# Sums of the down weights: from VectorE in one run to GpSimd in two, in the first block of a macaron layer

## The chip, the core and the metric

The kernel runs on one core of one Trainium2 chip. A core has TensorE (PE: matrix products into PSUM), VectorE (DVE), ScalarE (ACT) and GpSimd (POOL) for element-wise work, and SyncE (SP), whose queue issues every DMA of this kernel. Each engine works through its own instructions in the order in which they were written and waits on semaphores for the others. The metric is the device time of one execution in microseconds (us), lower is better; one other execution was taken with the hardware profiler.

## What is computed

Eight sequences of 512 tokens of width 512 pass through a gated feed-forward, attention, and the feed-forward again, each behind a layer norm and added to its input:

```python
x = x + 0.5 * ffn(layernorm(x));  x = x + attention(layernorm(x));  x = x + 0.5 * ffn(layernorm(x))

h = silu(x @ w_gate) * (x @ w_up)          # 512 -> 2048
h_sparse = the two of each four neighbours of h that are largest in magnitude
ffn = h_sparse @ w_down                    # 2048 -> 512
```

All of it is float32. The weights are the same for the sixteen feed-forwards.

## The kernel before

The work is cut into 16 blocks, one feed-forward of one sequence each. A block makes the hidden units in four parts (`c` = 0 to 3), and each part in two pairs (`i` = 2c and 2c + 1). A pair is seven products of eight matmuls (`woven`, L583): a Strassen-like scheme with seven products in place of eight, that works on four weight quarters (`Q11`, `Q12`, `Q21`, `Q22`) and on four sums of them (`S1` to `S4`). The very first pair is made plainly (`hidden`, L563). Three PSUM banks go round. Around the products, VectorE adds banks into a row and a corner (L608), multiplies (L157, the line of a helper that runs anything put off), and picks two of four (`keep_two_of_four`, L363 to L421), whose sums over halves of h (`e`) GpSimd makes (L415 to L420).

Two parts of h then go through the down weights with another seven products (`products`, L504), of sixteen matmuls each. These need, for each half `g` of the down weights, two quarters as they are and five sums of quarters (`SUMS`, L453). The sums are made once, in the first block: `combine_down` loads 1 MB of raw down weights, makes five sums of 128 x 512 float32, and writes each to memory (tile `wd`), four times over (`c` = 0 to 3; two times for each `g`). All later blocks read them from there (`down_weights`, L482). In the same way `combine_gu` (L656) makes `S1` to `S4` of the gate and up weights on VectorE, in the first block only, and stores them (tile `gu`).

The order of the instructions is written by a planner at build time. It keeps a modelled clock for PE, DVE and ACT (`at`), puts VectorE work into three queues (`urgent`, `put_off`, `for_later`), and after each product `fill` runs what fits by its estimate. GpSimd and DMAs have no clock in it. Side work (layer norms, attention, `combine_down`) is a generator that is advanced step by step between two places of the main work, given in half-products of 512 columns: the tuple for `combine_down` is (first place, last place, steps, ...), L960. The counter starts at 6.5 (L981); the first pair takes 4 places, every other pair 3.5, and a product with the down weights 1. Numbered from 0, pair 1 runs from 10.5, pair 2 from 14, pair 3 from 17.5, pair 4 from 21 and pair 5 from 24.5, with the first two down products woven in; the other five follow, and pair 6 begins at 35. `raw` lies in a ring of two buffers (`p_slots`), `sums` in one buffer (`wa_slots`), and the weight quarters `w` in a ring of sixteen (`load_quarters`, L106), so that the quarters of a pair are loaded into the buffers of the pair two before it, when that is done with them. In the first block VectorE reads these new quarters for the sums of the next pair while the present pair runs.

One line says how a sum was put on VectorE, one at a time and when it fits: `made = later(0.7, partial(combine, i, name), at["pe"], for_later)` (L477).

Of the kernel before, what the change touches and what calls it, by code (L numbers as in the profile page):

```python
# [26 lines left out]
def macaron_block(  # L27
# [12 lines left out]
    nc = tc.nc  # L40
# [3 lines left out]
    NCH = w_gu.shape[0]  # L44
# [96 lines left out]
    at = {"pe": 0.0, "dve": 0.0, "act": 0.0}  # L141
    urgent, put_off, for_later = deque(), deque(), deque()

    def takes(engine, us, ready=0.0):
        at[engine] = max(at[engine], ready) + us
        return at[engine]

    def pe_heard():
        return at["pe"] + HEARD
# [13 lines left out]
    def later(us, does, ready=None, queue=put_off):  # L163
        queue.append(Later(us, does, pe_heard() if ready is None else ready, queue))
        return queue[-1]

    def soon(us, does, ready=None):

        return later(us, does, ready, urgent)

    def ensure(entries):

        for entry in entries:
            while entry.end is None:
                entry.queue[0].run()
        return max((entry.end for entry in entries), default=0.0)
# [20 lines left out]
    p_slots = Slots(pp, "p", 2)  # L197
# [3 lines left out]
    wa_slots = Slots(wap, "wa", 1)  # L201
# [145 lines left out]
    def fill(slack=HEARD):  # L347

        while True:
            steps = thin["next"]  # L350
            for queue in (urgent, put_off, for_later):
                if queue and queue[0].fits(slack):
                    queue[0].run()
                    break
            else:
                if not steps or max(at["dve"], steps[1]) + steps[0] > at["pe"] + slack:
                    return
                step()
# [73 lines left out]
    def begin(steps):  # L432
# [2 lines left out]
        thin["steps"] = steps  # L435
        thin["next"] = next(steps)

    gu_made, written = {}, {}
    owed = []
    HD2 = D // 2  # L440
# [12 lines left out]
    SUMS = ("11+22", "12-22", "21-11", "11+12", "21+22")  # L453
    combined = {
        (g, name): dram.tile([P, 4, HD2], FP, name=f"wd_{g}_{i}")
        for g in range(NCH // 2)
        for i, name in enumerate(SUMS)
    }

    def combine_down():  # L460

        for c in range(NCH):
            raw = p_slots.tile([P, 4, D], FP, "raw")
            nc.sync.dma_start(out=raw, in_=w_down[c])
            there = at["pe"] + 12.0
            yield lambda: there
            yield now
            quarter = {f"{i + 1}{j + 1}": raw[:, i::2, j * HD2 : (j + 1) * HD2] for i in range(2) for j in range(2)}
            sums = wa_slots.tile([P, 6, 2, HD2], FP, "sums")

            def combine(i, name, c=c, quarter=quarter, sums=sums):
                op = ALU.add if name[2] == "+" else ALU.subtract
                nc.vector.tensor_tensor(sums[:, i], quarter[name[:2]], quarter[name[3:]], op)
                nc.sync.dma_start(out=combined[c // 2, name][:, c % 2 * 2 : c % 2 * 2 + 2, :], in_=sums[:, i])

            for i, name in enumerate(SUMS):
                made = later(0.7, partial(combine, i, name), at["pe"], for_later)  # L477
            p_slots.used(wa_slots.used(made))
            yield now
        ensure([made])  # L480

    def down_weights(g, name):  # L482
        w = wdp.tile([P, 4, HD2], FP, tag="wd", name="wd")
        if (g, name) in combined:
            nc.sync.dma_start(out=w, in_=combined[g, name])
        else:
            i = int(name[0]) - 1
            for q in range(2):
                nc.sync.dma_start(
                    out=w[:, 2 * q : 2 * q + 2, :], in_=w_down[2 * g + q][:, i::2, i * HD2 : (i + 1) * HD2]  # L490
                )
        return w

    def ffn(b, final, last):
# [5 lines left out]
        def store(xb, ts):  # L500
            for t in ts:
                nc.sync.dma_start(out=done[t * P : (t + 1) * P, :], in_=xb[:, t, :])

        def products(hs, g):  # L504

            operands = []

            def load():
                if len(operands) < len(PRODUCTS):
                    operands.append(down_weights(g, PRODUCTS[len(operands)][1]))  # L510

            def product(i):
                name, _, quarters = PRODUCTS[i]
                y = Bank([P, 2, HD2], "y")
                for t in range(2):
                    for n in range(4):
                        h, e = hs[n // 2]
                        if name in ("11+22", "21+22", "11+12"):
                            part = e[:, ("11+22", "21+22", "11+12").index(name), n % 2, :]
                        else:  # L520
                            row, col = int(name[0]) - 1, int(name[1]) - 1
                            part = h[:, 2 * (n % 2) + col, row * HALF : (row + 1) * HALF]
                        nc.tensor.matmul(  # L523
                            out=y.tile[:, t, :],
                            lhsT=part[:, t * P : (t + 1) * P],
                            rhs=operands[i][:, n, :],
                            start=(n == 0),
                            stop=(n == 3),
                        )
                takes("pe", 3.69)  # L530
                load()
                xb = xs[b, final]

                def add(half, side, sign, ends):
                    to = xb[:, 2 * half : 2 * half + 2, side * HD2 : (side + 1) * HD2]
                    nc.vector.scalar_tensor_tensor(to, y.tile, 0.5 * sign, to, ALU.mult, ALU.add)  # L536
                    if ends and g == NCH // 2 - 1 and i >= 5:
                        store(xb, (0, 1) if i == 5 else (2, 3))

                fill()  # L540
                y.free([soon(0.62, partial(add, *to, to == quarters[-1])) for to in quarters])
                written[b, final] = y.slot[1]

            for _ in range(3):
                load()
            return [(1 if i < 2 else 2, partial(product, i)) for i in range(len(PRODUCTS))]
# [129 lines left out]
        for c in range(NCH):  # L676
# [27 lines left out]
            else:  # L704
                for pair in range(2):
                    i = 2 * c + pair
# [25 lines left out]
            if plain:  # L732
                owed.extend((1 + t // 2, partial(down, h, w_plain, c, t)) for t in range(NT))
            elif c % 2:
                owed.extend(products(hs[-2:], c // 2))
# [221 lines left out]
        return WIDTH * blocks.index((b, i))  # L957


    sides = [(9, 25, 3 * NCH, combine_down, None, None)]  # L960
    for b, i in blocks[1:]:
        stage = partial(layernorm_t, normed[b, i], "xf", tokens[b][2 * i])
        sides.append((place(b, i) - 15, place(b, i) - 2, NORM, stage, ("attention", b) if i else None, None))
# [111 lines left out]
```

## Time and profile before

| | us |
|---|---|
| median of 3 runs | 3312.73 (3311.47 to 3315.4) |
| profiled execution | 3314.09, of which the span of instructions is 3312.3 |
| PE busy | 3224.5 (97% of the span) |
| DVE busy | 2293.9 (69%) |
| ACT busy | 1368.8 (41%) |
| POOL busy | 569.4 (17%) |
| first block's sums on DVE (L473) | 20, the first at 38.9, the last at 99.0 |

The page gives busy times of each engine over the whole span. A block lasts about 207 us (3312 / 16), so a change in the first block is read from the first part of the trace: the timeline lists each engine's instructions with start, duration, and in brackets how long the engine was idle before and what ended that.

### The profile page before, as it was taken

The numbers are of one execution on the slowest core, as the hardware profiler recorded it, in microseconds if no ns is written. First come the engines' busy times: TensorE is split into PE (matmuls) and PEld (weight loads), VectorE is DVE, ScalarE is ACT, GpSimd is POOL, SyncE is SP. The second block draws the span as 40 slices with busy tenths as digits, with TensorE's granted clock in tenths as the row PEclk, the third lists the DMA queues.
The fourth block names the chain that finished last, engine by engine and source line by source line (L and its number), as shares of the span: only waits on it lengthen the run. The fifth ranks groups of instructions, "written<-read, shape, count | busy, mean of one in ns | idle before, by whom it ended". The sixth has DMA issues, their size and how long they took to land.

```text
span 3312.3 us, 43741 instructions
## 1 busy us (share of the span) xinstructions
PE 3224.5 (97%) x15880; PEld 2322.0 (70%) x15880; DVE 2293.9 (69%) x4949; ACT 1368.8 (41%) x1841; POOL 569.4 (17%) x868
## 2 busy tenths in 40 slices
PE   8899999999999999999999999998999999999999
PEld 6787657765677667766776668765676668765786
DVE  6767865686577775777668865787568765786554
ACT  2222662246424562266324652256425552266221
POOL 0222002210130022111121112120120122101120
PEclk9999999999999999999999999999999999999999
DMA  7563333542344435334453345333533436333451
GB/s 254 186 234 102 109 120 119 175 140 96 116 165 140 131 116 185 127 120 132 142 171 123 121 142 193 128 113 104 189 103 131 140 123 205 100 122 118 138 172 48
DMA packets 249285, 463.21 MB, mean 140 GB/s; under 512 B 24432, under 2 KB 64368, under 8 KB 248304
## 3 DMA queue, kind: packets, MB, share of 16 engines
q1 hardware_dynamic: 249072, 460.42, 42.3%
q8 instruction: 127, 2.08, 0.3%
q14 instruction: 86, 0.70, 0.1%
HBM read 421.53 MB, written 38.80 MB: 139 GB/s over the span
## 4 chain that ended last, share of the span: by engine, by line
PE 84%; DVE 8%; ACT 4%; DMA 2%; issue 1%; POOL 1%; SPq 0%; DVEq 0%; ACTq 0%; POOLq 0%
PE x L594 22%; PE y L523 21%; PE v L594 11%; PE z L594 6%; PE proj L760 4%; PE sc L805 4%; PE ops L854 4%; PE st L838 4%; PE y L932 3%; DMA xn<-x 1%; PE tr L239 1%; PE gu L570 1%; ACT p L846 1%; PE den L872 1%; DVE p L157 1%
## 5 line engine op out<-in xcount | busy, mean ns | idle before, releaser
L594 PE MATMUL x<-ts,w 128*128 128x256 f32 x3000 | 726.3, 385 | 12.0 <-ACT row L224 6.5
L594 PEld LDWEIGHTS x<-ts,w 128*128 128x128 f32 x3000 | 562.1, 191 | 170.9 <-issue 55.7
L523 PE MATMUL y<-wd,h 128*128 128x256 f32 x1984 | 455.8, 384 | 8.2 <-DVE h L409 5.7
L523 PEld LDWEIGHTS y<-wd,h 128*128 128x128 f32 x1984 | 374.1, 191 | 100.7 <-issue 32.6
L157 DVE TENSOR_REDUCE nm<-sc 128x1 f32<-128x512 f32 x512 | 321.6, 683 | 87.9 <-PE sc L805 86.6
L415 POOL TENSOR_TENSOR e<-h 128x512 f32<-128x512 f32 x62 | 89.9, 1450 | 1664.3 <-DVE h L409 1502.8
L231 ACT ACT_TABLE_LOAD x290 | 372.1, 1283 | 5.8 <-PEq L1064 0.7
L523 PE MATMUL y<-wd,e 128*128 128x256 f32 x1488 | 336.9, 381 | 0.6 <-POOL e L417 0.5
L536 DVE SCALAR_TENSOR_TENSOR x<-y,x 128x512 f32<-128x512 f32 x372 | 242.4, 685 | 123.1 <-PE y L523 121.4
L523 PEld LDWEIGHTS y<-wd,e 128*128 128x128 f32 x1488 | 279.5, 190 | 62.9 <-issue 22.3
L846 ACT ACTIVATE p<-st 128x2048 f32<-128x2048 f32 x128 | 238.9, 1867 | 161.8 <-DVE p L157 91.2
L224 ACT COPY row<-x 128x512 f32<-128x512 f32 x166 | 96.9, 584 | 396.9 <-PE x L594 393.4
L157 DVE TENSOR_TENSOR p<-p 128x512 f32<-128x512 f32 x384 | 254.7, 717 | 6.1 <-PE ops L854 6.0
L594 PE MATMUL v<-ts,w 128*128 128x256 f32 x1000 | 241.2, 384 | 4.3 <-DVE w L661 3.7
L594 PE MATMUL z<-xT,w 128*128 128x256 f32 x1000 | 240.2, 383 | 3.8 <-PE tr L239 2.0
L594 PE MATMUL x<-xT,w 128*128 128x256 f32 x1000 | 241.0, 384 | 0.0
L594 PE MATMUL v<-xT,w 128*128 128x256 f32 x1000 | 239.8, 383 | 0.0
L594 PEld LDWEIGHTS v<-ts,w 128*128 128x128 f32 x1000 | 187.9, 191 | 54.4 <-issue 22.4
L594 PEld LDWEIGHTS x<-xT,w 128*128 128x128 f32 x1000 | 186.7, 191 | 55.2 <-issue 27.5
L594 PEld LDWEIGHTS z<-xT,w 128*128 128x128 f32 x1000 | 187.0, 191 | 53.6 <-issue 23.3
L594 PEld LDWEIGHTS v<-xT,w 128*128 128x128 f32 x1000 | 186.7, 190 | 51.2 <-issue 12.2
L371 ACT ACTIVATE a<-h 128x1024 f32<-128x1024 f32 x128 | 134.8, 1053 | 204.4 <-DVE m L389 114.0
(108 smaller groups left out, 4068.8 us busy)
## 6 DMA issues: line engine op xcount, KB each, us to landing
w<-gu SPq DMA_DIRECT2D x472, 256.0 KB, 3.3
w<-in_w_gu SPq DMA_DIRECT2D x394, 256.0 KB, 3.3
wd<-wd SPq DMA_DIRECT2D x155, 512.0 KB, 4.0
wd<-in_w_down SPq DMA_DIRECT2D x124, 256.0 KB, 5.2
x<-x SPq DMA_DIRECT2D x64, 256.0 KB, 2.6
xn<-x SPq DMA_DIRECT2D x64, 256.0 KB, 6.6
x<-in_x SPq DMA_DIRECT2D x32, 256.0 KB, 3.3
gu<-w SPq DMA_DIRECT2D x32, 256.0 KB, 2.6
```

The lines of the kernel that those rows point to most:

```text
L157: self.does()
L231: nc.scalar.activation(dummy[:, 1:2], dummy[:, 0:1], f)
L371: nc.scalar.activation(a, h[:, :, half * HALF : (half + 1) * HALF], AF.Abs)
L523: nc.tensor.matmul(out=y.tile[:, t, :], lhsT=part[:, t * P : (t + 1) * P], rhs=operands[i][:, n, :], start=(n == 0), stop=(n == 3),)
L536: nc.vector.scalar_tensor_tensor(to, y.tile, 0.5 * sign, to, ALU.mult, ALU.add)
L594: nc.tensor.matmul(out=bank.tile[:, m, :], lhsT=lhs[:, m, k, :], rhs=rhs[:, k, :], start=(first and m == 0 and k == 0), stop=(k == 1), ski ...
L760: nc.tensor.matmul(out=ps.tile, lhsT=wa[:, k, col : col + P], rhs=xT[:, k, :], start=(k == 0), stop=(k == ND - 1))
L805: nc.tensor.matmul(out=sc[:, kv, :], lhsT=qT[rows, c, t * P : (t + 1) * P], rhs=kT[rows, :], start=True, stop=True)
L838: nc.tensor.matmul(out=st[:, kv, :], lhsT=kT[rows, t * P : (t + 1) * P], rhs=qT[rows, c, :], start=True, stop=False)
L846: nc.scalar.activation(p, st, AF.Exp)
L854: nc.tensor.matmul(out=ops[rows, :], lhsT=v[:, t, rows], rhs=p[:, kv, :], start=(t == 0), stop=(t == NT - 1))
L932: nc.tensor.matmul(out=y.tile, lhsT=qT[:, k, t * P : (t + 1) * P], rhs=wo[:, k, :D], start=(k == 0), stop=(k == ND - 1))
```

## The change

`combine_down` gets an argument `g` and makes only the two chunks of that half. It runs as two sides: the first from place 11 to 18, the second from 22 to 32. In the order that is built, the five sums of chunks 0 and 1 stand in pairs 2 and 3, those of chunk 2 in pair 5, and those of chunk 3 among the five down products after it. The sums are issued at once, five in a row, on GpSimd and no longer through VectorE's queues; each is followed by its store, on SP as before. A set `done_down` makes the build fail if a product were written ahead of its sums. Buffers and sizes stay.

```diff
-    def combine_down():
-
-        for c in range(NCH):
+    def combine_down(g):
+
+        for c in range(2 * g, 2 * g + 2):
             raw = p_slots.tile([P, 4, D], FP, "raw")
             nc.sync.dma_start(out=raw, in_=w_down[c])
             there = at["pe"] + 12.0
...
             sums = wa_slots.tile([P, 6, 2, HD2], FP, "sums")
 
-            def combine(i, name, c=c, quarter=quarter, sums=sums):
+            for i, name in enumerate(SUMS):
                 op = ALU.add if name[2] == "+" else ALU.subtract
-                nc.vector.tensor_tensor(sums[:, i], quarter[name[:2]], quarter[name[3:]], op)
-                nc.sync.dma_start(out=combined[c // 2, name][:, c % 2 * 2 : c % 2 * 2 + 2, :], in_=sums[:, i])
-
-            for i, name in enumerate(SUMS):
-                made = later(0.7, partial(combine, i, name), at["pe"], for_later)
-            p_slots.used(wa_slots.used(made))
+                nc.gpsimd.tensor_tensor(sums[:, i], quarter[name[:2]], quarter[name[3:]], op)
+                nc.sync.dma_start(out=combined[g, name][:, c % 2 * 2 : c % 2 * 2 + 2, :], in_=sums[:, i])
             yield now
-        ensure([made])
+        done_down.add(g)
...
-    sides = [(9, 25, 3 * NCH, combine_down, None, None)]
+    sides = [(11, 18, 6, partial(combine_down, 0), None, None), (22, 32, 6, partial(combine_down, 1), None, None)]
```

## The prediction

> **What bounds the kernel now.** I read first the busy times of the page, then who waited for whom on PE in the first block alone, then the timelines of PE and DVE there.
>
> ```profile
> span 3312.3 us, 43741 instructions
> PE 3224.5 (97%) x15880; PEld 2322.0 (70%) x15880; DVE 2293.9 (69%) x4949; ACT 1368.8 (41%) x1841; POOL 569.4 (17%) x868
> ```
>
> PE is the bound over the span, so only what stops PE counts. The built orders of both kernels differ in the first block alone: every engine's list is the same, line numbers aside, from the second block on. So I ask what PE loses there. The waits of PE between 24 and 142 us:
>
> ```profile
> PE y L523 <- DVE h L409: 5.7, 2, 3.0
> PE v L594 <- DVE w L661: 3.7, 1, 3.7
> PE x L594 <- DVE corner L608: 3.5, 1, 3.5
> PE z L594 <- DVE h L157: 1.7, 1, 1.7
> ```
>
> All are waits for DVE, 14.7 us together (3.52 + 1.71 + 3.73 + 2.79 + 2.96 in the PE timeline). From that timeline:
>
> ```profile
> 48.41 1.89 PE L594 MATMUL z<-xT,w 128*128 128x256 f32 x8
> 53.81 3.78 PE L594 MATMUL x<-ts,w 128*128 128x256 f32 x8 [3.52 <-DVE corner L608]
> 57.39 3.02 PE L594 MATMUL x<-xT,w 128*128 128x256 f32 x8
> 60.24 1.89 PE L594 MATMUL v<-ts,w 128*128 128x256 f32 x8
> ```
>
> After the wait eight matmuls take 3.78 and then 3.02 us, not 1.89: a wait costs more than its length. Undisturbed, eight start every 1.727 us (29.41 to 48.41 us: 19.00 / 11). From 27.69 us (pair 1) to 142.84 (first transpose in pair 6) stand 53 such eights: 39 of L594 and 14 of L523. 53 x 1.727 = 91.5 of 115.15 us, so **23.6 us are lost**: 14.7 waiting and 8.9 in slow matmuls. That is the most the change can win, 0.7%. DVE's timeline says why:
>
> ```profile
> 42.31 2.49 DVE L473 TENSOR_TENSOR sums<-raw 128x512 f32<-128x512 f32 x4
> 49.94 2.02 DVE L661 TENSOR_TENSOR w<-w 128x512 f32<-128x512 f32 x3 [5.14 <-DMA w<-in_w_gu]
> ...
> 96.55 3.10 DVE L473 TENSOR_TENSOR sums<-raw 128x512 f32<-128x512 f32 x5 [0.68 <-DMA wd<-sums]
> ```
>
> Twenty sums take 14.2 us of DVE (12.1 at 0.604 start to start); DVE also waits for quarters that SP issued at 40.45, behind the store of a sum (39.56) and 1 MB of raw weights (39.94).
>
> **What the Trainium skill says.** "SBUF — State Buffer", section "SBUF: two separate sides": DVE and GpSimd share a port pair under an exclusive lock; a DVE op with two SBUF inputs and a GpSimd op exclude each other for the whole instruction. The trace agrees: in the timeline from 501 us
>
> ```profile
> 502.67 1.27 POOL L418 TENSOR_TENSOR e<-h 128x512 f32<-128x512 f32 x1
> 502.70 3.46 DVE L157 TENSOR_TENSOR p<-p 128x512 f32<-128x512 f32 x2
> 503.90 1.71 POOL L419 TENSOR_TENSOR h<-h 128x512 f32<-128x512 f32 x1
> 505.57 1.72 POOL L420 TENSOR_TENSOR h<-h 128x512 f32<-128x512 f32 x1
> 506.08 0.68 DVE L608 TENSOR_TENSOR corner<-x,corner 128x512 f32<-128x512 f32 x1
> ```
>
> the two engines alternate: two DVE sums take 3.46 us (1.3 alone), POOL starts 1.67 apart. The add from PSUM (L608, 0.68) isn't touched. So one GpSimd sum delays one such DVE op by 1.67 - 0.60 = 1.07 us. "GPSIMD Engine Reference", section "Elementwise — side-by-side cycle accounting": a two-input sum costs 1.96 times DVE's. Here 1.27 (L417 alone) against 0.60. "TensorE: Matmul & The Clock Gate", section "What's actually happening": after some 3.4 us of idleness the clock halves until PE is busy again. Here waits of 2.8 to 3.7 us cost another 1.6 to 3.0, and the wait of 1.71 us nearly nothing.
>
> **The change part by part.** Times are the new kernel's own; PE runs pair 1 at 27.7, pair 2 at 39.8, pair 3 at 51.9, pair 4 at 64.0 and pair 5 at 76.0 if it never waits. The last product of a pair needs DVE's corner add within 10.36 us (6 x 1.727) of the pair's start.
>
> *Removed from DVE:* 20 sums, 12.1 us, and their waits for stores. POOL now has these waits (the second five await the stores of the first). Behind them on POOL stand only the sums `e` and layer-norm scales, below.
>
> *Chunk 0.* Raw follows the quarters of pair 2, at 26.7 us (they ended at 26.63); median landing 6.2, so at 33 to 35. Five sums to about 41. They delay w (35.5), h-corner and h-row on DVE by about 1 each. Corner is done at 37.7, due 38.05; row copy at 42.4, due 43.2. Cost 0. The quarters of pair 3 no longer have raw or a sum's store ahead and land near 45; DVE, which now picks two of four first, asks at 45.3. Corner of pair 2: 49.3, due 50.1. So the **first wait, 3.52 + 3.1 slow, goes: 6.6 won.**
>
> *Chunk 1.* On POOL its sums follow the first `e`, which waits for L409, at 54.5 us. Raw is issued at 47.7 and there by 54. So six POOL ops start as DVE runs, from 54.5: L384, L386, L388, L389, four small bf16 ops, three w sums, row, w, two small, corner. Alone these are 2 x 0.60 + 2 x 0.34 + 0.8 + 3 x 0.60 + 0.6 + 0.6 + 0.4 + 0.6 = 6.7, corner at 61.2, due 62.2. With six ops pushed by 1.07 each it is 67.6: **a new wait of 5.4, and about 2.3 slow (the mean of 1.6 and 3.0): 7.7.** Bounds: nothing, if DVE keeps the lock; 9. I take the alternation of 502 us. What is late next: L417 to L420 then meet the h-row and L384 of pair 4: 0.7 more.
>
> *Chunk 2.* The same place in pair 5: `e` and five sums from L409 on (2.6 after the pair's start). Row add, which frees the bank for the down product y of `e`, alone at 2.6 + 5.1 = 7.7, now 14.1; due at 12.1 (four products, one down product of 3.45 and another of 1.73). **Wait 2.0, then 0.6 for the next bank, and 1.5 slow: 4.1** (0 to 6). The half of h that y takes is ready 4 us early, so both L409 waits go.
>
> *Chunk 3.* Its sums run among five down products in a row, whose adds read PSUM and have two products, 6.9 us, of slack; about five DVE ops late by 1.07: cost 0 (to 2).
>
> *Nothing elsewhere,* each with its cover. `e` of chunk 2's part waits 5 sums on POOL, done 7 us before its product; without that cover 1.2 each. Scales of the next layer norm are done at about 110 + the waits above, transposes come at 119 + the same. On SP all 20 stores move: they wait for POOL, and the quarters of pair 5 stand behind chunk 1's five stores. Those issue at 65 to 69, but the quarters also wait for PE's last product of pair 3, itself late. The down weights' loads follow, 15 us before use. Loads of raw stay four.
>
> Sum: 23.6 lost before; after, 7.7 + 0.7 + 4.1 = 12.5 plus about 0.5 of small gaps = 13.0. **Gain 10.6**: span 3312.3 - 10.6 = 3301.7. The profiled run is 3314.09, 1.4 above the median of 3312.73, so the median becomes **3302.1**.
>
> **Rivals.** A change within 0.2% (6.6 us) can't be told from none.
>
> *Whole relief.* DVE keeps the lock, or the delays fall into its idle time; PE waits 3 or less: gain 20 to 23, 3290 to 3293. For it: DVE ops of 0.28 in bf16 at 299 us weren't delayed by a running POOL op. Against: L386 beside POOL ops took 1.72 in all 16 cases, not 0.68.
>
> *Transfers stay late.* About 27 MB must move in some 100 us, not 119: near 270 GB/s, where the busiest stretch (60 to 80 us) reached 323. Were the quarters of pairs 3, 5 and 6 each late by 2 to 3, 7 would come on top: gain 3.6, 3309, no change.
>
> *Slower: the lock takes it all.* Twenty sums can push DVE by 20 x 1.07 = 21.4, and four waits that each slow the clock add 4 x 2.3 = 9.2; with all on PE's path 30.6 against 23.6, 3320. It decides from 14 of 20 on the path (15.0 + 9.2 = 24.2). Against: chunks 0 and 3 have slack.
>
> That the sums don't move is excluded: the built order has them on POOL.
>
> **Chances.** Forecast (gain 7 to 16, 3297 to 3306) 0.51; whole relief 0.20; no change 0.20; slower 0.09. So faster by over 0.2% 0.71, within 0.20, slower 0.09. The forecast alone holds 0.51; with most of the relief (from 3290) and two thirds of the no-change case (to 3312) it is 0.8: 3290 to 3312.
>
> **What would show it.** Right: no PE wait for corner near 50 us; POOL sums at 33 to 41, from 56, from about 90 and 108; L386, L389 and w of pairs 3 and 5 at 1.4 to 1.8 us; PE waits of 4 to 6 for corner in pair 3 and 2 to 3 for a bank in pair 5; the transpose of pair 6 near 132, not 142.8. Wrong: DVE idle in front of w for DMA; DVE ops at 0.68 beside POOL sums; or a difference that arises after 150 us, where the orders agree.

## The result and the profile after

The changed kernel takes **3307.01 us** (median of 13 runs, 3304.48 to 3311.98) against 3315.90 for the kernel before beside it (13 runs, 3310.70 to 3318.39): ratio 0.9977, 95% interval 0.9969 to 0.9986, so 8.9 us less. The profiled execution took 3308.2 us with a span of 3306.1, which is 6.2 less than the span of before. Runs of one kernel lie up to 5 us either side of their median, so a span and a median do not agree to better than that.

The first lines of the page after:

```profile
span 3306.1 us, 43735 instructions
PE 3220.5 (97%) x15880; PEld 2320.0 (70%) x15880; DVE 2293.0 (69%) x4929; ACT 1369.4 (41%) x1841; POOL 600.5 (18%) x888
```

Twenty instructions have moved from DVE to POOL, and DVE's busy time has fallen by 0.9 us, not by the 14.2 that these twenty took. What each wait of PE in the first block was for, from 24 to 150 us of the kernel after (total, times, longest):

```profile
PE x L592 <- DVE corner L606: 5.4, 1, 5.4
PE y L521 <- issue: 2.1, 1, 2.1
PE y L521 <- DMA wd<-wd: 1.9, 1, 1.9
PE y L521 <- DVE x L534: 1.3, 1, 1.3
PE tr L239 <- DVE row L606: 1.1, 1, 1.1
PE x L592 <- ACT row L224: 0.5, 1, 0.5
```

All five waits of before are gone and others stand in their place. The fourth is put down to DVE, but the wait was for a load, as is shown with chunk 3 below. Line numbers past L504 are 2 lower than before, those between L475 and L504 3 lower. PE's timeline after (start, length, then what it waited for just before):

```profile
61.09 1.89 PE L592 MATMUL z<-xT,w 128*128 128x256 f32 x8
68.38 3.78 PE L592 MATMUL x<-ts,w 128*128 128x256 f32 x8 [5.40 <-DVE corner L606]
71.95 2.94 PE L592 MATMUL x<-xT,w 128*128 128x256 f32 x8
74.73 1.89 PE L592 MATMUL v<-ts,w 128*128 128x256 f32 x8
...
100.20 5.38 PE L521 MATMUL y<-wd,e 128*128 128x256 f32 x16 [2.12 <-issue]
105.41 1.89 PE L592 MATMUL z<-xT,w 128*128 128x256 f32 x8
...
117.80 3.69 PE L521 MATMUL y<-wd,e 128*128 128x256 f32 x16 [1.87 <-DMA wd<-wd]
122.81 7.14 PE L521 MATMUL y<-wd,h 128*128 128x256 f32 x32 [1.32 <-DVE x L534]
...
136.70 0.60 PE L239 MATMUL tr<-ident,xn 128*128 128x128 f32 x4
```

Pair 1 starts at 28.07 and the first transpose of pair 6 comes at 136.70: 108.63 us. The same 53 eights at 1.727 are 91.5, so **17.1 us are lost where before lost 23.6**: 11.2 waiting (5.40 + 0.47 + 2.12 + 1.87 + 1.32) and 5.9 in slow matmuls. That is 6.5 us won in this stretch. At equal instructions of DVE the lead over before is 5.3 us at 163 us (the 1.1 us for DVE's row in pair 6 lie behind the stretch), 6.9 at 480, between 6.2 and 8.6 after that, and 6.2 at the end: most of it arises in the first block, and later it goes up and down in steps of up to 1.7 us.

DVE's timeline after shows where the corner of pair 3 is held up:

```profile
54.99 0.69 DVE L384 TENSOR_TENSOR m<-a 128x512 bf16<-128x512 f32 x1
55.60 1.75 DVE L386 TENSOR_TENSOR m<-a 128x512 bf16<-128x512 f32 x1
57.28 1.49 DVE L388 TENSOR_TENSOR m<-a 128x256 bf16<-128x256 f32 x1
58.69 1.48 DVE L389 TENSOR_TENSOR m<-a 128x256 bf16<-128x256 f32 x1
60.10 1.35 DVE L394 TENSOR_TENSOR m<-m 128x256 bf16<-128x256 bf16 x1
61.37 1.35 DVE L395 TENSOR_TENSOR m<-m 128x256 bf16<-128x256 bf16 x1
62.65 1.35 DVE L397 TENSOR_TENSOR m<-m 128x256 bf16<-128x256 bf16 x1
63.92 0.28 DVE L398 TENSOR_TENSOR m<-m 128x256 bf16<-128x256 bf16 x1
...
67.65 0.68 DVE L606 TENSOR_TENSOR corner<-x,corner 128x512 f32<-128x512 f32 x1
...
99.41 0.68 DVE L606 TENSOR_TENSOR row<-v,row 128x512 f32<-128x512 f32 x1
```

and POOL's timeline what runs beside it:

```profile
55.03 1.77 POOL L415 TENSOR_TENSOR e<-h 128x512 f32<-128x512 f32 x1 [13.17 <-DMA w<-in_w_gu]
56.77 7.08 POOL L474 TENSOR_TENSOR sums<-raw 128x512 f32<-128x512 f32 x5
```

Six POOL instructions, six DVE instructions at 1.75, 1.49, 1.48 and three times 1.35, each 1.07 over its own length of 0.68, 0.42, 0.41 and 0.28. When POOL has finished, the seventh (L398) is back at 0.28. The same picture stands in pair 5. There the wait of 2.12 has no releaser in the view ("issue"), but it ends 0.11 us after DVE's row add (99.41 to 100.09), which frees the bank: the text calls it the bank wait. Twelve instructions delayed by 1.063 to 1.071 in pairs 3 and 5, with three smaller delays in pair 1, make 14.5 us: as much as the removed sums took.

### The profile page after: what moved, and what is told of

Its sections match the earlier page's. It is cut to its first block, busy times and chain, and to the rows that moved or that the text cites. A ratio compares the mean times of both kernels' runs of the same rounds, so it can differ in the third digit from the quotient of the medians.

```text
span 3306.1 us, 43735 instructions
## 1 busy us (share of the span) xinstructions
PE 3220.5 (97%) x15880; PEld 2320.0 (70%) x15880; DVE 2293.0 (69%) x4929; ACT 1369.4 (41%) x1841; POOL 600.5 (18%) x888
## 4 chain that ended last, share of the span: by engine, by line
PE 85%; DVE 6%; ACT 4%; DMA 2%; issue 1%; POOL 1%; SPq 0%; DVEq 0%; ACTq 0%; POOLq 0%
PE x L592 23%; PE y L521 21%; PE v L592 11%; PE z L592 6%; PE proj L758 4%; PE sc L803 4%; PE ops L852 4%; PE st L836 4%; PE y L930 3%; PE tr L239 1%; PE gu L568 1%; ACT p L844 1%; DMA xn<-x 1%; PE den L870 1%; PE vps L783 1%
## 5 line engine op out<-in xcount | busy, mean ns | idle before, releaser
L415 POOL TENSOR_TENSOR e<-h 128x512 f32<-128x512 f32 x62 | 90.8, 1465 | 1602.3 <-DVE h L409 1417.8
L632 ACT ACTIVATE h<-corner 128x256 f32<-128x256 f32 x125 | 51.7, 414 | 408.8 <-DVE corner L606 408.5
```

## The experiments

The change does two things: it puts the sums on another engine, and it puts them at other places. The theory on test was that of the prediction: the moved place removes the first wait, the shared port lock of DVE and POOL takes part of that back. Its rival for the gain: that it comes of relieving DVE. "Lost" is PE's time from pair 1 to the first transpose of pair 6, less 91.5 us; it is from one profiled execution each. What is left of the span when "lost" is taken off lies between 3285.7 and 3292.2 us in the twelve profiles, so "lost" and the medians agree to a few us only. Kernels are edited from the changed one, unless said otherwise.

| kernel | engine | places | median us | ratio to before (95%) | lost us |
|---|---|---|---|---|---|
| before | VectorE | old | 3314.6 to 3315.9 | 1 | 23.6 |
| changed | GpSimd | new | 3307.0 | 0.9977 (0.9969–0.9986) | 17.1 |
| places alone | VectorE | new | 3300.2, 3300.5 | 0.9955 (0.9941–0.9970), 0.9956 (0.9943–0.9968) | 10.5, 10.2 |
| GpSimd alone | GpSimd | old | 3312.9 | 0.9994 (0.9986–1.0003) | 20.2 |
| fills for sums | GpSimd | new | 3300.1 | 0.9955 (0.9938–0.9971) | 5.2 |
| sums twice | GpSimd | new | 3324.3 | 1.0030 (1.0019–1.0041) | 31.6 |
| old side, two places later | VectorE | 11 to 25 | 3307.8 | 0.9981 (0.9973–0.9989) | 14.3 |
| first half early | GpSimd | 6.5, 22 | 3306.2 | 0.9976 (0.9966–0.9985) | 12.5 |
| both halves moved | GpSimd | 6.5, 27 | 3301.0 | 0.9962 (0.9949–0.9974) | 8.4 |
| half on each | both | 6.5, 22 | 3302.9 | 0.9971 (0.9960–0.9983) | 10.2 |
| VectorE, second half late | VectorE | 11, 27 | 3301.6 | 0.9958 (0.9944–0.9972) | 7.2 |

### The places alone

```diff
+            def combine(i, name, c=c, quarter=quarter, sums=sums):
...
+                nc.vector.tensor_tensor(sums[:, i], quarter[name[:2]], quarter[name[3:]], op)
...
-                nc.gpsimd.tensor_tensor(sums[:, i], quarter[name[:2]], quarter[name[3:]], op)
...
+                made = later(0.7, partial(combine, i, name), at["pe"], for_later)
+            p_slots.used(wa_slots.used(made))
...
+        ensure([made])
```

> The new places (two sides, 11 to 18 and 22 to 32) with the sums still on VectorE, put off one by one as before. If the gain of the change comes from taking twenty sums off VectorE, this loses most of it: 3311 to 3320, with PE waiting again for VectorE in the pairs in which sums stand. If the gain comes from the place alone (no raw weights ahead of the quarters of pair 3), it is near the changed kernel, 3304 to 3309, and the wait of 3.5 us near 50 us is gone all the same.

It took 3300.24 us (4 runs), less than either expectation had it, and once more:

> The run with the changed places and all sums on VectorE once more, in more rounds: 3299 to 3303 again, 5 to 8 below the changed kernel, if its four runs were typical; within 3 of the changed kernel if they were not.

3300.53 us (5 runs), as expected. **With the sums left on VectorE the new places win 14.3 and 15.4 us, more than the whole change.** PE's waits in the first block (24 to 150 us) of the first of these kernels:

```profile
PE x L597 <- DVE corner L611: 3.4, 2, 2.1
PE v L597 <- ACT corner L224: 1.6, 1, 1.6
PE y L526 <- DVE h L409: 1.5, 1, 1.5
PE v L597 <- DVE w L664: 1.3, 1, 1.3
PE y L526 <- DMA wd<-wd: 1.0, 1, 1.0
```

Six waits add up to 8.7 us, not far below the 11.2 of the changed kernel. But none is longer than 2.1, and the matmuls behind them are at full speed: the sum of 10.5 lost leaves 1.8 for slow ones, where the changed kernel has 5.9. Part of that is chance. The second profile of the same kernel has the same wait of 2.06 us, and there the matmuls behind it are slow (the first line is of the first profile, the others of the second):

```profile
67.22 1.99 PE L597 MATMUL x<-ts,w 128*128 128x256 f32 x8 [2.06 <-DVE corner L611]
...
66.28 3.06 PE L597 MATMUL x<-ts,w 128*128 128x256 f32 x8 [2.06 <-DVE corner L611]
69.13 2.55 PE L597 MATMUL x<-xT,w 128*128 128x256 f32 x8
```

It waits 6.9 us and loses 3.3 in slow matmuls, 10.2 in all. Against the kernel before, the new places win more than the first wait: where before waited 3.7 us for w and 5.7 for h, this kernel waits 1.3 and 1.5. One thing is not separated: through the queue the sums are also spread between other instructions of DVE, five in a row no longer in all chunks. No run has them on VectorE five in a row at the new places.

### GpSimd alone

```diff
-    sides = [(11, 18, 6, partial(combine_down, 0), None, None), (22, 32, 6, partial(combine_down, 1), None, None)]
+    sides = [(9, 25, 3 * NCH, combine_down, None, None)]
```

with `combine_down` again over four chunks.

> GpSimd makes the sums, at the old places (one side, 9 to 25). The sums of chunk 1 then stand ahead of the first e on GpSimd, and those of chunks 2 and 3 about e of the second part. By the lock theory each group of five delays VectorE by up to 5.4 us wherever it runs, so there are again waits of 2 to 6 us in two of the pairs 2 to 5: 3303 to 3312. If the place decides, the raw weights stand ahead of the quarters of pair 3 as before and the wait near 50 us comes back: 3310 to 3316.

3312.85 us (12 runs), as expected if the place decides: ratio 0.9994, the interval holds 1. The three largest entries among PE's waits in the first block and, below, the line of DVE that comes ahead of the longest wait (5.39 us, up to 55.76 us, in pair 2):

```profile
PE x L593 <- DVE corner L607: 6.3, 2, 5.4
PE x L593 <- ACT row L224: 4.7, 1, 4.7
PE y L522 <- issue: 2.3, 1, 2.3
...
```

```profile
49.00 4.03 DVE L660 TENSOR_TENSOR w<-w 128x512 f32<-128x512 f32 x3 [3.84 <-DMA w<-in_w_gu]
```

DVE waits 3.84 us for the quarters of pair 3, much as it waited 5.14 before, since the raw weights go out right ahead of them again; and then three sums that take 2.0 us alone take 4.03, with POOL's sums beside them. So the old place keeps the old wait whichever engine makes the sums.

### The old side two places later

To try the place in its smallest form, one number of the kernel **before** was changed:

```diff
-    sides = [(9, 25, 3 * NCH, combine_down, None, None)]
+    sides = [(11, 25, 3 * NCH, combine_down, None, None)]
```

> The kernel before, with the first place of its one side at 11 instead of 9 and nothing else, so that the first raw load stands behind the quarters of pair 2 and the second behind those of pair 3. If the gain of the new places comes from the quarters no longer queued behind 1 MB of raw weights, VectorE's wait of 5.1 us near 50 us and PE's 3.5 go: 3303 to 3310. If it comes from splitting the work in two sides with a gap between, most of the 14 us remain lost: 3311 to 3317.

3307.80 us (13 runs), 6.8 less than before, within what was expected if the queue of quarters decides. By the intervals in the table this one number can't be told from the whole change. It moves the sums themselves too, so the raw load's place is not tried alone; but with GpSimd alone, DVE's wait for the quarters stayed without any sums on DVE. The corner wait of pair 2 is gone, and DVE no longer waits for the quarters at 49 us. Of the 12.6 us that PE still waits there, 5.06 are one new wait. The two longest in pairs 3 and 4, in PE's timeline of this kernel:

```profile
67.00 1.99 PE L594 MATMUL x<-ts,w 128*128 128x256 f32 x8 [1.67 <-DVE corner L608]
75.78 3.75 PE L594 MATMUL v<-ts,w 128*128 128x256 f32 x8 [5.06 <-DVE w L661]
```

### The lock: fills, and every sum twice

Three fills stand for one sum, at the same places on the same engine. The kernel leaves the sums out; stores and transfers stay.

```diff
-                nc.gpsimd.tensor_tensor(sums[:, i], quarter[name[:2]], quarter[name[3:]], op)
+                for _ in range(3):
+                    nc.gpsimd.memset(sums[:, i], 0.0)
```

> As the changed kernel, but each sum is replaced by three fills of the same tile with zeros on GpSimd, so GpSimd is busy for about as long at the same places of its queue, and the stores wait for it in the same way, but it reads nothing from SBUF; the sums are left out. By the lock theory VectorE's operations beside them take 0.68 us again, the waits of 5.4 us in pair 3 and 2.1 us in pair 5 go with their slow matmuls (2.9 and 1.8): 12 us less than the changed kernel, about 3295. If the waits come from GpSimd being busy, or from the stores and quarters queued behind it on SP, they stay and the time is about 3307.

3300.12 us (4 runs), 6.9 below the changed kernel; in the first block PE loses 5.2 us, 11.9 less. The first block thus gives the 12 us expected, the time only 6.9 of them; where the rest went the runs do not show. POOL's timeline there, and DVE's beside it:

```profile
57.50 8.20 POOL L475 MEMSET sums<- 128x512 f32 x15
```

```profile
56.35 1.76 DVE L386 TENSOR_TENSOR m<-a 128x512 bf16<-128x512 f32 x1
58.03 0.41 DVE L388 TENSOR_TENSOR m<-a 128x256 bf16<-128x256 f32 x1
...
59.51 2.01 DVE L660 TENSOR_TENSOR w<-w 128x512 f32<-128x512 f32 x3
```

POOL is busy for longer than with the sums (8.20 against 7.08 us), yet DVE runs at its own speed; only L386, which starts beside POOL's `e`, still takes 1.76. The corner wait and the bank wait are gone. This agrees with the Trainium skill, "SBUF — State Buffer", section "SBUF: two separate sides", which has a DVE instruction with two SBUF inputs excluded only by a GpSimd instruction that reads SBUF. The run shows that it is not GpSimd's being busy that costs, nor the stores and loads. That it is the sums' reading is argued from that page: a fill differs from a sum in more than this, and it doesn't wait for the raw weights.

The other direction:

```diff
                 nc.gpsimd.tensor_tensor(sums[:, i], quarter[name[:2]], quarter[name[3:]], op)
+                nc.gpsimd.tensor_tensor(sums[:, i], quarter[name[:2]], quarter[name[3:]], op)
```

> As the changed kernel, but GpSimd makes every sum twice. By the lock theory five more operations of VectorE are pushed by 1.07 us in each group: the wait for the corner in pair 3 grows from 5.4 to about 10.7, the one for the bank in pair 5 from 2.1 to about 7.5, and chunk 0 may cost 1 to 4: 3317 to 3323. If the length of the sums is hidden and the waits have another cause, 3306 to 3309.

3324.34 us (7 runs), 17.3 above the changed kernel, slower than before and a little more than expected. The corner wait grew to 8.9 us (10.7 expected), that for the bank to 4.1 (7.5 expected): 29 delayed instructions of DVE, 29.1 us, of which fewer than reckoned stand ahead of those two adds. Waits for ACT's row copies (7.3 us in three), not foreseen, took the place.

### Other places for the sums

The first half earlier, so that the sums meet less of pair 3:

```diff
-    sides = [(11, 18, 6, partial(combine_down, 0), None, None), (22, 32, 6, partial(combine_down, 1), None, None)]
+    sides = [(6.5, 13, 6, partial(combine_down, 0), None, None), (22, 32, 6, partial(combine_down, 1), None, None)]
```

> As the changed kernel, but the first side starts at place 6.5 and ends at 13, so the raw weights of chunk 0 are loaded at the start and the sums of chunks 0 and 1 run on GpSimd in pairs 0 and 1, ahead of the first e. VectorE has slack there: in the changed kernel the sums of chunk 0, in pair 1, made PE wait for nothing. Lock theory: no wait for the corner in pair 3 (5.4 us and 2.9 of slow matmuls go), the bank wait in pair 5 stays near 2: about 8.5 less than the changed kernel, 3296 to 3301. If it is the number of sums on GpSimd and not their place that costs, 3305 to 3309.

3306.22 us (9 runs, 3300.57 to 3309.45): not to be told from the changed kernel, and a miss. In the profile the corner wait is gone, with its slow matmuls, but waits for ACT's row copies (3.8 us in two) and for down weights (2.6) came, and the first block is 4.6 us shorter and not 8.5. That execution, of 3300.57, was the lowest of the nine, and it had luck: the bank wait of pair 5 is there at its old length, and this time sixteen matmuls behind it run at full speed (3.69 us, in the changed kernel 5.38):

```profile
97.22 3.69 PE L521 MATMUL y<-wd,e 128*128 128x256 f32 x16 [2.12 <-issue]
```

Behind a wait for ACT of 2.55 us, in pair 4, matmuls run at full speed too. The other executions may have lost 1.7 us or so behind each of these; they were not profiled.

The wait of 2.55 itself can be followed: ACT's row copy stands behind its magnitudes (L371), which waited until 75.98 us for DVE's L389; ahead of that, L384 and L386 had taken 1.78 and 1.75 us beside GpSimd's L419 and L420. It is the same delay of DVE, from GpSimd's work that the change did not touch.

The second half later as well, `(27, 40, 6, partial(combine_down, 1), None, None)`:

> As v1, and the second side from 27 to 40, so that the sums of chunk 2 run after the e of the second part and those of chunk 3 in pair 6 or later. Lock theory: the bank wait in pair 5 goes as well (2.1 and 1.8), but the sums of chunk 3 may now meet VectorE's work of pairs 6 and 7, where a wait of up to 5 comes back: 3292 to 3301, about 3296. If transfers bound the first block by now, no faster than v1.

3300.98 us (5 runs), within the expected range. Bank wait and wait for down weights go too. What is left in its first block, most of it behind ACT's copies:

```profile
PE x L592 <- ACT row L224: 5.1, 2, 2.6
PE tr L239 <- DVE row L606: 1.2, 1, 1.2
PE x L592 <- DVE row L226: 0.3, 1, 0.3
```

The first half early on GpSimd and the second on VectorE through the queue, at 22 to 32:

```diff
...
+                engine = nc.vector if g else nc.gpsimd
+                engine.tensor_tensor(sums[:, i], quarter[name[:2]], quarter[name[3:]], op)
...
```

> As v1 for chunks 0 and 1 (GpSimd, early); chunks 2 and 3 at the places of the changed kernel, but on VectorE through its queue. Lock theory: no corner wait in pair 3, no bank wait of 2.1 in pair 5, small waits of 1 to 1.5 us that leave the matmuls at full speed instead, as seen with all sums on VectorE at the new places: 3294 to 3300. If GpSimd at the old places costs no more than VectorE does, equal to v1.

3302.94 us (7 runs, 3297.70 to 3307.38): above the range expected, and by the intervals not to be told from the early first half with all sums on GpSimd.

And places alone, on VectorE, with the second half at 27 to 40:

> All sums on VectorE, the first side at 11 to 18, the second at 27 to 40. Pair 5 and the down products then hold no sums of chunk 2: of the 8.7 us that PE still waits in the first block with all sums on VectorE at the changed places, 1.3 (corner of pair 5... its sums' share), 1.5 (h of L409) and 1.0 (late down weights) should go; sums of chunk 3 in pair 6 or 7 may bring back 1 to 2: 3296 to 3301, about 2 below the same with the second side at 22 to 32. If sums simply move their waits along, the two are equal within 2.

3301.64 us (5 runs), 1.1 to 1.4 above the places alone and not 2 below. Its first block loses 7.2 us, 3 less than with the places alone, which the time doesn't show: runs of one kernel differ by more. These, both halves moved and the places alone lie within 1.4 us of each other; the runs don't rank them. **The places alone, on VectorE, are the simplest of these that beats both kernels.**

## Why the prediction was right

Forecast were 3302.1 us and a gain of 10.6; measured were 3307.0 and 8.9 between the medians. Of the 4.9 us between the two times, 3.2 are the kernel before, whose median beside these runs was 3315.9 and not the 3312.73 of three runs; 1.7 are a smaller gain. Step by step:

- *Chunk 0, first wait won (6.6).* Right. No wait for a corner stands near 50 us, the sums run at 35.04 to 41.86, and DVE does not wait for quarters ahead of pair 3's w. The two-places edit of the kernel before removes the same wait and wins 6.8.
- *Chunk 1, a wait of 5.4 and 2.3 slow.* The wait was 5.40. The two eights behind it took 6.35 us (68.38 to 74.73), 2.9 more than 3.45; the granted clock was 0.51 there (67.2 to 74.1 us). The delays made the wait, as reckoned, but not all six delayed instructions were those expected: the three w sums, taken for some of them, ran at 0.68 each, and the four small bf16 instructions, three of them at 1.35, paid instead. The count of six, and so the sum, held.
- *Chunk 2, a wait of 2.0, then 0.6, and 1.5 slow.* The wait was 2.12, the slow part 1.8 (5.21 from 100.20 to 105.41, for 3.45; granted clock 0.50 from 101.4 to 104.8 us); no further wait for a bank came. The wait was reckoned; that the slow part came at all was luck, as behind the same 2.12 us the early first half lost nothing more.
- *Chunk 3, cost 0 (to 2), and "nothing elsewhere".* **Here stands the term that was mis-sized.** The five down products' adds made PE wait for nothing, as reckoned. But PE waited 1.87 and 1.32 us there, 3.2 together, for down weights from memory. The view puts the second wait down to DVE's x add:

```profile
121.53 1.29 DVE L534 SCALAR_TENSOR_TENSOR x<-y,x 128x512 f32<-128x512 f32 x2 [2.66 <-PE y L521]
```

But DVE had itself been waiting for PE, and its second add ended at 122.82, when PE had already gone on (122.81); the first ended at 122.2. The load of that product's weights, issued at 115.06, landed 7.6 us later, near 122.7: that is what PE waited for. The forecast's "15 us before use" is said of the loads behind the quarters of pair 5; these went out by 75.80 and were used from 92.74 us without a wait. For the later loads it gave no cover. SP's queue after:

```profile
104.96 0.42 SPq L465 DMA_DIRECT2D raw<-in_w_down  x1
105.43 3.26 SPq L259 DMA_DIRECT2D xn<-in_x  x4
108.80 0.50 SPq L482 DMA_DIRECT2D wd<-wd  x1
...
115.06 1.24 SPq L482 DMA_DIRECT2D wd<-wd  x2
```

The 512 KB issued at 108.80, behind 1 MB of raw weights and four loads of the next tokens, took 8.9 us to land; PE could have used them at 115.9 (117.80 - 1.87), 7.1 us after the issue. In this stretch (100 to 118 us) the 16 DMA engines had hardly a gap. Packets, MB and share of the engines:

```profile
q1 hardware_dynamic: 3087, 6.25, 97.9%
```

In the kernel before it was 3.84 MB and 69.6% between the same times. The places alone, on VectorE, have such a wait too (1.0 and 0.7 us in its two profiles), and the second half at 27 has none: it goes with the place of the second half and not only with GpSimd. Why it is longer with GpSimd (3.2) is open. This is the rival "transfers stay late" in a small form; its own places, the quarters of pairs 3, 5 and 6, were not late.
- *Sum.* 17.1 us are still lost in the trace and not 13.0: 3.2 of the 4.1 between them in chunk 3, and 0.9 in slow matmuls (2.9 and 1.8 against 2.3 and 1.5); the smaller terms, as the 0.7, the 0.6 and the gaps, cancel. The first transpose of pair 6 came at 136.70 and not near 132, of which 0.4 is the later start of pair 1. The trace therefore gives 6.5 in the first block for the 8.9 of the medians; the rest is within the spread of single runs.
- *Removed from DVE, 12.1 us.* The count is right, and as a source of gain it is empty: the two engines in one place differ against GpSimd at the new places (17.1 lost to 10.5), and not measurably at the old ones. The forecast listed these sums as removed and put no gain on them by name; it didn't work out what the new places alone would give, and so missed that at these places the change of engine costs more than it brings.
- *The rivals.* Whole relief is out, since the delays are there and at full length. (The 1.72 us of L386 "in all 16 cases" is a mean: fifteen took 1.75 to 1.77, one 1.17.) The lock alone doesn't reach the loss that would make the kernel slower, as the doubled sums show what that takes: 29 delayed instructions instead of 15, and 8 more us lost than before.

Two things stay open: where the 4.6 us of the early first half went between its profile and its median, and why the fills' gain in the first block shows in their time only in part.

## What to carry to other kernels

When a change moves work in time and to another engine at once, cost the two apart: here the place won some 15 us and the engine took about 6 of them back. Whether sums spread out on GpSimd would have cost less was not tried. A two-input sum on GpSimd is no relief for a VectorE that reads two SBUF inputs at that time, as each cost VectorE up to 1.07 us where its own sum costs 0.60; look for a place that does not send a megabyte ahead of a transfer that is soon due. In these first blocks several waits under 2 us were cheaper than one of the same sum, as no matmuls were slow behind them.

## What was not expected of the hardware

- The small bf16 instructions, 0.28 us alone, were held up to 1.35, by as much as the longer ones beside GpSimd's sums. The delay, 1.063 to 1.071 us in twelve cases, did not depend on the length or type of the DVE instruction. The forecast took those at 299 us in the kernel before, undelayed at 0.28, for a sign that they might escape; there it was GpSimd that waited, as its L415 took 2.03 us.
- The lock is not shared evenly: beside DVE's instructions five sums of POOL took 7.08 us, among down products 6.30. POOL lost 0.16 us by each on average (a sum took from 1.31 us beside DVE's shortest instructions to 1.72 beside its longest, 1.27 alone), DVE 1.07.
- Behind a wait of middle length, slow matmuls are a matter of chance. From 24 to 150 us of the twelve profiles, none of the 31 waits from 0.5 to 2.0 us was followed by slow matmuls, 8 of the 14 from 2.06 to 2.58 were, and all 11 from 2.79 to 8.94. Nor does the loss grow with the wait: the first eight took 3.78 us after 3.52, after 5.40 and after 8.94. The Trainium skill, "TensorE: Matmul & The Clock Gate", section "What's actually happening", puts the idle window at about 3.4 us and calls it free-running: it doesn't reset with the kernel's start. That fits one wait of 2.06 us with two outcomes, but no run here shows the window itself.
- POOL's fills took 0.55 us each (8.20 / 15) and delayed nothing of DVE's.
